# The last narrow block of gate and up, computed as one full mixed block and a half block multiplied directly

## The chip, the cores and the metric

The kernel runs on one core of a Trainium2 chip. The time is device microseconds (us) of one launch, the median of three runs. A profiled execution is a run of its own, with its own time. Engines are named as in the profile: PE (TensorE, matrix products; PEld is its weight load), DVE (VectorE), ACT (ScalarE), POOL (GpSimd) and SP (SyncE, which mostly issues DMAs).

## The reference

One decoder layer on x of 16 batches × 128 tokens × 1024 features, all in f32. Each of three parts normalises x, computes, and adds to x: a self-attention of width 256, a cross-attention with a softmaxed context, and a gated feed-forward with weights stored as 4-bit codes. The change is in the last:

```python
Wg = dequantize(gate_Wq, gate_scale, gate_zero)   # [2752, 1024], (code - zero) * scale
Wu = dequantize(up_Wq, up_scale, up_zero)         # [2752, 1024]
Wd = dequantize(down_Wq, down_scale, down_zero)   # [1024, 2752]
g = jnp.einsum('bsh,ih->bsi', x, Wg)
u = jnp.einsum('bsh,ih->bsi', x, Wu)
h = jax.nn.silu(g) * u
return jnp.einsum('bsi,hi->bsh', h, Wd)
```

So there are 2048 tokens, 1024 inputs, 2752 intermediate columns in each of gate and up, and 1024 outputs.

## The kernel before

The attention parts come first. Beside them DVE begins to dequantize weights and to store them, with the sums that are needed of them, in DRAM (`prepare`). The normalised rows are turned and stored in two halves of 1024 tokens, called passes here.

**Products with seven multiplications.** Where a product of 2 × 2 blocks would take eight block products, the kernel takes seven (Winograd's form of Strassen's scheme), at the price of sums of the operands and of the results. `GATE` (line 39) is the order of the seven for gate and up, `DOWN` (line 40) that for down. For gate and up the 2 × 2 blocks are two halves of the tokens (512 each), two halves of the inputs (512 each, four chunks of 128) and two halves of a block of columns. `BLOCKS` (line 41) cuts the 2752 columns into ten blocks of 2 × 128 and an eleventh of 2 × 96; the eleventh is `RB = 10` with half width `RW = 96`.

**First pass.** `one_block` (line 1084) computes each of the eleven blocks: 14 products, seven for gate and seven for up (`SEQUENCE`), each of four matmuls of 512 tokens into a PSUM bank (`products`, line 1044; the matmul is line 1063). A matmul call is two PE instructions in the profile. ACT copies partial results (`keep`), DVE adds, ACT applies Silu, DVE multiplies. The results h go to DRAM as `h_all[block, 1 or 2, token half]`. PE runs in an order written out by hand, and so does DVE here (`tensor` and `vector` are wrapped in `InOrder`). After each product `beside` (line 1383) does a step of other work: at first what is left of the attention (`tick`), then a step of `prepare`, and in the last block the operands of the second pass (`outer_operand`, `inner_right`).

**Weights.** `load_weights` (line 976) loads a tile of two products' weights, and runs `AHEAD = 4` tiles ahead of `next_tile`. Four tiles are loaded before the first block (line 1377), on SP's queue like nearly every load and store.

**Second pass.** For the ten full blocks the scheme is applied twice (`two_levels`, line 1190): blocks in pairs, 35 outer products (`OUTERS`), each with seven inner products of 256 tokens (their instructions stand under line 52, in the wrapper). POOL makes the weights' sums (`inner_left`, tiles li), DVE those of the tokens (`inner_right`, tiles ti), and `got` and `finish` put the results together on DVE and ACT. Those that serve several pairs (`KEPT`, line 1134) are made once, at the pair's first use: while outer product n runs, the sums for n + 1 go to the list `soon_due`, which is worked off between the inner products (`do_extra`), as is a second list, `extra`. After the outer products, `one_block` runs once more for the eleventh block, and at its end makes the four sums of h that down wants (`combine_h`, line 1013) from the first pass's h, reloaded into tiles hl, and its own. Sums of the last pair of full blocks that are left over are worked off by the second `beside` (line 1413), one after each product; at its third call that function also issues the first 25 loads of down (`operands`, line 902).

**Down.** Seven outer products (`DOWN`), each with seven inner products (`INNER`) of five pairs of full blocks, for which DVE makes the operands' sums (`combine`, line 1452). The eleventh block enters once per outer product with the tiles of `remainder` (line 1442), one more matmul pair in four of the inner products, which needs `h_all[10, q]` for that outer product's q.

**What sets the order.** Within an engine's stream, instructions that are not pinned in program order are placed by a planner that works with its own estimates; its costs are not shown. Its decisions can be read only from the order in the trace. SP's queue and POOL's are such streams. PE in down is one too.

Of the kernel before, what the change touches and what calls it, by code (L numbers as in the profile page):

```python
# [11 lines left out]
F32 = mybir.dt.float32  # L12
# [28 lines left out]
BLOCKS = [(b * 2 * P, min(P, (INTER - b * 2 * P) // 2)) for b in range(-(-INTER // (2 * P)))]  # L41

# [13 lines left out]
def decoder_layer(  # L56
# [100 lines left out]
    def load_raw(blk, mat, s):  # L157
# [10 lines left out]
        q, szs = (gq, gsz) if mat == "g" else (uq, usz)  # L168
        off = start + s * w
        raw = raw[:, : JC * w].rearrange("p (j f) -> p j f", j=JC)  # L170
        nc.sync.dma_start(raw, q[:, :, ds(off, w)])

        sz = pools["sz"].tile([P, 2 * P], F32, name="sz")[:, : 2 * w]
        nc.sync.dma_start(sz, szs[:, ds(2 * off, 2 * w)])
        scale, zero = (m.unsqueeze(1).to_broadcast([P, JC, w]) for m in (sz[:, :w], sz[:, w:]))
        return raw, scale, zero

    def prepare(jobs, ahead, queue, vector=nc.vector):


        units = [(blk, mat, s) for blk, mat in jobs for s in range(2)]
# [7 lines left out]
        for k, (blk, mat, s) in enumerate(units):  # L189
            w = BLOCKS[blk][1]  # L190
            size = [w, 512] if mat == "d" else [P, JC * w]
# [25 lines left out]
            yield  # L217
            if s == 0:
                continue
# [667 lines left out]

    RB = len(BLOCKS) - 1
    RW = BLOCKS[RB][1]
# [4 lines left out]
    h_all = {}  # L894

# [36 lines left out]
    with ExitStack() as gs:  # L932
# [9 lines left out]
        def attention_done():  # L942
# [5 lines left out]
            for blk in range(EARLY, len(BLOCKS)):  # L948
                jobs += [(blk, "g"), (blk, "u")]
                if blk >= EARLY + 2:  # L950
                    jobs.append((blk - EARLY - 2, "d"))
# [10 lines left out]
        SEQUENCE = [(mat, q) for mat in "gu" for q in GATE]  # L962

        def tiles_of(blk):
            todo = [(blk, *k) for k in SEQUENCE]
            return [todo[n : n + 2] for n in range(0, len(todo), 2)]
# [9 lines left out]
        def load_weights():  # L976
            if to_load:
                wt = cw.tile([P, 2, 512], F32, name="w")
                for n, (blk, mat, q) in enumerate(to_load.popleft()):
                    cols = slice(0, JC * BLOCKS[blk][1])  # L980
                    nc.sync.dma_start(wt[:, n, cols], wprep[blk, mat][GATE.index(q)])
                loaded.append(wt)
# [5 lines left out]
        def next_weights(w):  # L988
            if not waiting:
                wt = next_tile()  # L990
                waiting.extend(
                    wt[:, n, : JC * w].rearrange("p (j f) -> p j f", j=JC) for n in range(2)
                )
# [5 lines left out]
        def store(blk, q, half, t, delay=2):  # L999
            if (blk, q, half) not in h_all:  # L1000
                w = BLOCKS[blk][1]
                h_all[blk, q, half] = dram.tile(
                    [w, TB], F32, name=f"h{blk}_{q}{half}", tag=f"h{blk}_{q}{half}"
                )
            stores.append([delay, h_all[blk, q, half], t])
# [38 lines left out]
        def products(blk, mat, T, got):  # L1044

            w = BLOCKS[blk][1]
            bank, kept = {}, {}

            def keep(q, ps):
                t = kept[q] = ct.tile([P, TB], F32, name="k", tag=f"k{q}", bufs=2 if q == 1 else 1)  # L1050
                t = kept[q] = t[:w]
                nc.scalar.copy(t, ps)  # L1052

            def product(q):
                wt = next_weights(w)
                put_stores()
                first = {6: 1, 5: 1, 3: 1, 4: 7}.get(q, q)
                if first == q:
                    banks.rotate(1)
                    bank[q] = banks[0].tile([P, TB], F32, name=f"p{q}", tag="gu")[:w]  # L1060
# [23 lines left out]
        def one_block(ps, blk, T, between):  # L1084

            w = BLOCKS[blk][1]
            sg, hs, first_h = {}, {}, {}

            def gate(k, bank, add):
                t = sg[k] = ct.tile([P, TB], F32, name="sg", tag="sg")[:w]  # L1090
# [6 lines left out]
            def up(k, bank, add):  # L1097
                t = hs[k] = ch.tile([P, TB], F32, name="h", tag="h")[:w]
# [6 lines left out]
                if ps == 0:  # L1105
                    store(blk, 1 + n, half, t)
                    return
                if n == 1:
                    store(blk, 4, half, t)
                if (1 - n, half) in hs:  # L1110
                    for step in combine_h(
# [553 lines left out]
```

## Time and profile before

| | |
|---|---|
| time, median of 3 runs (lowest to highest) | 2329.98 us (2327.83 to 2329.99) |
| the profiled execution's own time | 2327.36 us |
| its span | 2325.4 us |
| PE busy | 2291.2 us, 99% |
| DVE, ACT, POOL busy | 1559.1, 557.3, 388.3 us |
| DMA | 424.69 MB, mean 183 GB/s |
| first pass, gate and up (from the wait for the first weights to the last block's end) | about 806 to 1370.8 us |
| of it the eleventh block | 1322.7 to 1370.8 us |
| second pass, outer products | 1370.8 to 1800.5 us |
| second pass, eleventh block | 1800.5 to 1848.6 us |
| down | 1848.6 to 2325.4 us |

Times in the trace count from the start of the span. A row of the timeline gives start, duration, engine, line, operation, tiles written and read, the count of instructions merged, and in brackets the engine's idle time before it with what ended it. PE's durations overlap, since matmuls are pipelined: what one costs is the step from one start to the next. A row of a table of waits gives who waited for whom, the total, how often, and the longest.

### The profile page before, as it was taken

What the parts mean: (1) busy time and instruction counts of PE and PEld (TensorE: products, weight loads), DVE (VectorE), ACT (ScalarE), POOL (GpSimd) and SP (SyncE); (2) the same over time, 40 slices, a digit from 0 to 9 for tenths busy, and PEclk for the clock granted to TensorE, in tenths of its full rate; (3) what the DMA queues carried; (4) which work ended last, traced back from release to release, by engine and by line L of the source; (5) the groups of instructions that cost most, each with busy time, mean ns of one, the idle gap of its engine ahead of it and who ended that gap; (6) DMA issues with size and microseconds to landing.
All of it is one profiled execution on the core that took longest, in us unless ns stands there. A gap on an engine that the chain in (4) does not pass through costs nothing.

```text
span 2325.4 us, 25297 instructions
## 1 busy us (share of the span) xinstructions
PE 2291.2 (99%) x8976; PEld 1585.3 (68%) x8976; DVE 1559.1 (67%) x2224; ACT 557.3 (24%) x891; POOL 388.3 (17%) x281
## 2 busy tenths in 40 slices
PE   8999999999999899999999999999999999999999
PEld 7556557667666564444444457888888488888888
DVE  6694788888888816776767547777777455443462
ACT  2111255565565551111111111222111100000000
POOL 5120122222222200000000023444443000000000
PEclk9999999999999999999999999999999999999999
DMA  6242365666676558787889733554554965434631
GB/s 242 66 132 89 109 172 172 179 183 181 180 220 207 166 147 260 253 286 258 276 265 317 249 95 98 198 173 140 196 195 131 322 193 160 158 124 146 218 113 37
DMA packets 275774, 424.69 MB, mean 183 GB/s; under 512 B 26752, under 2 KB 124928, under 8 KB 275520
## 3 DMA queue, kind: packets, MB, share of 16 engines
q1 hardware_dynamic: 256544, 398.16, 54.2%
q10 hardware_dynamic: 16800, 16.52, 2.3%
q0 software_dynamic: 2304, 8.39, 0.9%
q8 instruction: 72, 1.18, 0.2%
q14 instruction: 54, 0.44, 0.1%
HBM read 265.62 MB, written 157.35 MB: 182 GB/s over the span
## 4 chain that ended last, share of the span: by engine, by line
PE 93%; DVE 3%; DMA 1%; issue 1%; ACT 0%; SPq 0%; POOL 0%; DVEq 0%; ACTq 0%; POOLq 0%
PE p L1063 24%; PE po L1552 20%; PE q L52 17%; PE mm L52 11%; PE kq L52 8%; PE mm L367 5%; PE tr L52 3%; PE mm L382 2%; PE mm L263 2%; PE tr L314 1%; DMA kh<-kd 1%; DVE bnst L52 0%; DMA wo_again<-in_wo 0%; DVE kt L52 0%; DVE qmx L52 0%
## 5 line engine op out<-in xcount | busy, mean ns | idle before, releaser
L1063 PE MATMUL p<-b,w 128*128 128x512 f32 (+1 forms) x768 | 340.0, 595 | 6.0 <-DMA w<-wg 6.0
L1063 PEld LDWEIGHTS p<-b,w 128*128 128x128 f32 (+1 forms) x768 | 142.8, 186 | 191.7 <-issue 187.8
L1063 PE MATMUL p<-T,w 128*128 128x512 f32 (+1 forms) x576 | 255.5, 592 | 0.0
L1063 PEld LDWEIGHTS p<-T,w 128*128 128x128 f32 (+1 forms) x576 | 106.6, 186 | 138.7 <-issue 136.6
L52 PE MATMUL q<-ti,li 128*128 128x256 f32 x840 | 194.6, 382 | 4.2 <-DVE ti L52 4.2
L1552 PE MATMUL po<-wc,lc 128*128 128x256 f32 x840 | 183.4, 379 | 0.0
L52 POOL TENSOR_TENSOR li<-w 128x512 f32<-128x512 f32 x70 | 94.4, 1350 | 531.1 <-PE p L1063 476.5
L52 PEld LDWEIGHTS q<-ti,li 128*128 128x128 f32 x840 | 160.4, 191 | 27.4 <-issue 5.3
L1552 PEld LDWEIGHTS po<-wc,lc 128*128 128x128 f32 x840 | 159.6, 190 | 21.8
L683 POOL TENSOR_TENSOR qe<-qe,qden 128x1024 f32<-128x1024 f32 x64 | 121.6, 1899 | 266.8 <-DVE qden L52 231.8
L52 ACT COPY k<-q 128x512 f32<-128x512 f32 x105 | 61.4, 585 | 345.4 <-PE q L52 345.4
L52 DVE TENSOR_TENSOR pa<-pa,sz 128x512 f32<-128x512 int32 (+3 forms) x176 | 129.6, 737 | 5.5
L1552 PE MATMUL po<-wq,lq 128*128 128x256 f32 x560 | 126.7, 379 | 0.2 <-issue 0.2
L52 PE MATMUL mm<-kh,cxt 128*128 128x256 f32 x512 | 122.6, 382 | 3.6 <-DMA kh<-kd 3.3
L52 PE MATMUL kq<-cx,wk_sb 128*128 128x512 f32 x256 | 120.7, 594 | 4.0 <-ACT ke L640 3.5
L1052 ACT COPY k<-p 128x512 f32<-128x512 f32 (+1 forms) x72 | 42.1, 584 | 342.8 <-PE p L1063 342.8
L52 PEld LDWEIGHTS mm<-qs,m_sb 128*128 128x128 f32 x512 | 97.2, 190 | 38.9 <-issue 28.0
L52 PE MATMUL kq<-wq_sb,xn 128*128 128x512 f32 x256 | 120.5, 593 | 0.0
L52 PE MATMUL mm<-qs,m_sb 128*128 128x256 f32 x512 | 120.3, 379 | 0.0
L52 PEld LDWEIGHTS mm<-kh,cxt 128*128 128x128 f32 x512 | 95.9, 190 | 33.6 <-issue 19.6
L52 DVE TENSOR_REDUCE qmx<-kq 128x16 f32<-128x1024 f32 x64 | 76.3, 1193 | 63.0 <-PE kq L52 62.9
L1552 PEld LDWEIGHTS po<-wq,lq 128*128 128x128 f32 x560 | 106.0, 190 | 15.9 <-issue 0.8
(176 smaller groups left out, 3687.6 us busy)
## 6 DMA issues: line engine op xcount, KB each, us to landing
w<-wg SPq DMA_DIRECT2D x140, 256.0 KB, 3.0
w<-wu SPq DMA_DIRECT2D x140, 256.0 KB, 3.5
lq<-h SPq DMA_DIRECT2D x140, 256.0 KB, 4.5
kd<-kt SPq DMA_DIRECT2D x64, 512.0 KB, 3.5
kh<-kd SPq DMA_DIRECT2D x128, 256.0 KB, 5.5
h<-hc SPq DMA_DIRECT2D x80, 256.0 KB, 2.9
wq<-wd SPq DMA_DIRECT2D x70, 256.0 KB, 5.3
h<-h SPq DMA_DIRECT2D x60, 256.0 KB, 3.0
```

The source lines that it names most:

```text
L52: return lambda *args, **kw: self._tc.keep_in_program_order(fn(*args, **kw))
L263: tensor.matmul(ps, oT[:, d, ts(b % BPT, S)], wo_d[d][:, ts(h, 512)], start=(d == 0), stop=(d == 1),)
L314: nc.tensor.transpose(tr[:, j, :], xn[:, ts(4 * h + j, P)], ident)
L367: nc.tensor.matmul(ps[:, tokens], wqkv_sb[:, f, c, :], xnT[:, c, tokens], start=(c == 0), stop=(c == CC - 1),)
L382: nc.tensor.matmul(ps, xnT[:, c, ts(i, S)], wqkv_sb[:, 4:6, c, :], start=(c == 0), stop=(c == CC - 1),)
L683: nc.gpsimd.tensor_tensor(qe, qe, den.unsqueeze(2).to_broadcast(wide), ALU.mult)
L1052: nc.scalar.copy(t, ps)
L1063: nc.tensor.matmul(ps, wt[:, j, :], T[q][:, j, :], start=(first == q and j == 0), stop=(q in (2, 3, 4) and j == JC - 1), skip_group_check= ...
L1552: nc.tensor.matmul(bank[:, i, :], l[:, ts(i, S)], w,  start=(start and c == 0 and i % 2 == 0), stop=(stop and c == len(pairs) - 1), skip_g ...
```

## The change

The eleventh block is split in another way. Of gate's 192 columns and of up's 192, the first 128 of each form one block of full width ("m"): gate's 128 are its first half, up's 128 its second. It takes seven products instead of fourteen. The 64 + 64 columns left (`REST`) form a single tile of 128 columns ("r"), which is multiplied directly: `half_product` runs four times, for two token halves and two halves of the inputs, using the token block T[5] = (block − T[1]) so that the second half of the tokens can be added to a copy of the first. In "r" the rows of gate and up lie in different partitions: gate's 64 rows go through Silu and are shifted by a DMA on ACT's queue from partitions 0 to 63 to partitions 64 to 127, and there multiplied with up's. Columns are ordered accordingly on the host, and `prepare` has one unit for "r" and two for "m" in place of four.

The sums of this block's h for down are no longer made at the end of the second pass. All its h go to DRAM (the second pass's under the keys "e" and 4), and `last_combinations` loads them in down's first outer product, once after its inner product 7 and once after 3, makes the sums on DVE and stores them from ACT's queue.

With the block shorter, the calls of `between` change: nine per block instead of fourteen, two after parts of "r" and one after each product of "m". `beside`'s work is keyed to those. Down's first loads still come at the third call.

Two more edits: the first tile of weights of the first pass is loaded from POOL's queue instead of SP's, and the sums `inner_right(T, 4)` are put on the list `extra` in outer product n = 4, where before they came with n = 5.

The diff, cut to its core:

```diff
+RB = len(BLOCKS) - 1
+RW = BLOCKS[RB][1]
+REST = 2 * RW - P
+SUBS = [(start + s * w, w) for start, w in BLOCKS[:RB] for s in range(2)]
+SUBS += [(BLOCKS[RB][0], P), (BLOCKS[RB][0] + P, REST)]
...
+        if mat == "r":
+            parts = [(m, *SUBS[-1]) for m in "gu"]
+        elif mat == "m":
+            parts = [("gu"[s], *SUBS[-2])]
+        else:
+            parts = [(mat, start + s * w, w)]
+        at = 0
+        for m, off, w in parts:
+            q, szs = matrices[m]
+            nc.sync.dma_start(raw[:, :, ds(at, w)], q[:, :, ds(off, w)])
...
-        units = [(blk, mat, s) for blk, mat in jobs for s in range(2)]
+        units = [(blk, mat, s) for blk, mat in jobs for s in range(1 if mat == "r" else 2)]
...
+            if mat == "r":
+                out = wprep[blk, mat] = dram.tile([2, *size], F32, name="wr0", tag="wr0")
+                for n in range(2):
+                    stores.append((out[n], A[0, n]))
...
-                jobs += [(blk, "g"), (blk, "u")]
+                jobs += [(blk, mat) for mat in ("gu" if blk < RB else "rm")]
...
+        LAST = [("r", n) for n in range(2)] + [("m", q) for q in GATE]
         def tiles_of(blk):
-            todo = [(blk, *k) for k in SEQUENCE]
+            todo = [(blk, *k) for k in (SEQUENCE if blk < RB else LAST)]
...
-        def load_weights():
+        def load_weights(queue=nc.sync):
             if to_load:
                 wt = cw.tile([P, 2, 512], F32, name="w")
-                for n, (blk, mat, q) in enumerate(to_load.popleft()):
-                    cols = slice(0, JC * BLOCKS[blk][1])
-                    nc.sync.dma_start(wt[:, n, cols], wprep[blk, mat][GATE.index(q)])
-                loaded.append(wt)
+                todo = to_load.popleft()
+                for n, (blk, mat, q) in enumerate(todo):
+                    queue.dma_start(wt[:, n], wprep[blk, mat][q if mat == "r" else GATE.index(q)])
+                loaded.append((wt, len(todo)))
...
-                if ps == 0:
-                    store(blk, 1 + n, half, t)
-                    return
-                if n == 1:
-                    store(blk, 4, half, t)
-                if (1 - n, half) in hs:
-                    for step in combine_h(
-                        blk,
-                        half,
-                        first_h[1, half],
-                        first_h[2, half],
-                        hs[0, half],
-                        hs[1, half],
-                        vector,
-                    ):
-                        step()
...
+            make = {"g": products(T, gate), "u": products(T, up)}
             for n, (mat, q) in enumerate(SEQUENCE):
                 make[mat](q)
-                if ps == 1 and n == 5:
-                    hl = xres.tile([P, 2, 2, TB], F32, name="hl", tag="X6")
-                    for half in range(2):
-                        for k in (1, 2):
-                            t = first_h[k, half] = hl[:w, k - 1, half]
...
                 between(n, mat, q)
+        def last_block(ps, T, between):
+            keys = {0: (1, 2), 1: ("e", 4)}[ps]
+            bank, up, done = {}, {}, {}
+            todo = deque()
+            def put(half, t, first, row, n):
+                parity = keys[n]
+                store(RB, parity, half, t[first], row=row)
+            def small(half, x, u):
+                g = ct.tile([P, TB], F32, name="sg", tag="sg")
+                nc.scalar.activation(g[:REST], x[:REST], AF.Silu)
+                nc.scalar.dma_start(g[ds(REST, REST)], g[:REST])
+                def mult():
+                    rows = ds(REST, REST)
+                    t = ch.tile([P, TB], F32, name="h", tag="h")
+                    vector.tensor_tensor(t[rows], u[rows], g[rows], ALU.mult)
+                    put(half, t, rows, 0, 1)
+                todo.append(mult)
+            def half_product(p, w, q, start, stop):
+                for j in range(JC):
+                    nc.tensor.matmul(
+                        bank[p],
+                        w[:, j, :],
+                        T[q][:, j, :],
+                        start=(start and j == 0),
+                        stop=(stop and j == JC - 1),
+                        skip_group_check=True,
+                    )
+            put_stores()
+            ws = [next_weights() for _ in range(2)]
+            for p in range(2):
+                banks.rotate(1)
+                bank[p] = banks[0].tile([P, TB], F32, name=f"p{p}", tag="gu")
+            half_product(0, ws[0], 1, True, False)
+            k = ct.tile([P, TB], F32, name="k", tag="k1", bufs=2)
+            nc.scalar.copy(k, bank[0])
+            between(0, "r", 0)
+            half_product(1, ws[1], 2, True, True)
+            c0 = ct.tile([P, TB], F32, name="sg", tag="sg")
+            vector.tensor_tensor(c0, bank[1], k, ALU.add)
+            small(0, c0, c0)
+            put_stores()
+            half_product(0, ws[0], 5, False, False)
+            between(1, "r", 1)
+            half_product(0, ws[1], 3, False, True)
+            small(1, bank[0], bank[0])
+            def finish(half, t):
+                put(half, t, slice(0, RW), 0, 0)
+                put(half, t, slice(RW, P), REST, 1)
+            def got(k, ps, add):
+                n, half = k
+                if k == (1, 1):
+                    t = up[half] = ch.tile([P, TB], F32, name="h", tag="h")
+                    vector.tensor_tensor(t, ps, add, ALU.add)
+                elif k == (1, 0):
+                    t = ch.tile([P, TB], F32, name="h", tag="h")
+                    vector.tensor_tensor(t, ps, add, ALU.add)
+                    vector.tensor_tensor(t, t, done[half], ALU.mult)
+                    finish(half, t)
+                else:
+                    t = done[half] = ct.tile([P, TB], F32, name="sg", tag="sg")
+                    if add is None:
+                        nc.scalar.activation(t, ps, AF.Silu)
+                        vector.tensor_tensor(t, up[half], t, ALU.mult)
+                        finish(half, t)
+                    else:
+                        vector.tensor_tensor(t, ps, add, ALU.add)
+                        nc.scalar.activation(t, t, AF.Silu)
+            make = products(T, got)
+            for n, q in enumerate(GATE):
+                make(q)
+                between(2 + n, "m", q)
+                if todo:
+                    todo.popleft()()
...
                     soon_due.extend(inner_right(T, OUTERS[n + 1][1]))
                 if n == 0:
                     extra.append(lambda: outer_operand(T, 4))
+                elif n == 4:
+                    extra.extend(inner_right(T, 4))
...
-        for _ in range(AHEAD):
-            load_weights()
+        for n in range(AHEAD):
+            load_weights(nc.gpsimd if n == 0 else nc.sync)
...
             if blk == RB:
-                for k in {("g", 1): (5,), ("g", 2): (7,), ("u", 6): (6,)}.get((mat, q), ()):
+                for k in {("r", 0): (5,), ("r", 1): (7,), ("m", 6): (6,)}.get((mat, q), ()):
                     outer_operand(T1, k)
-                if (mat, q) == ("u", 1):
+                if (mat, q) == ("m", 1):
                     for step in inner_right(T1, 1):
                         step()
...
             if blk == RB:
                 blocks.update(pass1)
-            one_block(0, blk, T, beside)
+                last_block(0, T, beside)
+            else:
+                one_block(blk, T, beside)
...
-        one_block(1, RB, T1, beside)
+        last_block(1, T1, beside)
...
+        def last_combinations(half):
+            h = {}
+            for q in (4, "e", 1, 2):
+                h[q] = dh.tile([P, TB], F32, name="dh")[:RW]
+                nc.sync.dma_start(h[q], h_all[RB, q, half])
+            for q, dst, a, b, op in (
+                (5, 4, "e", 4, ALU.add),
+                (7, "e", 1, "e", ALU.subtract),
+                (6, 1, 4, 1, ALU.subtract),
+                (3, 2, 2, 1, ALU.subtract),
+            ):
+                nc.vector.tensor_tensor(h[dst], h[a], h[b], op)
+                new_h(RB, q, half)
+                nc.scalar.dma_start(h_all[RB, q, half], h[dst])
...
                 ps = bank[set_]
                 multiply(ps, pairs, set_ == iq, iq == 6 or more is not None)
                 put_outs()
+                if n == 0 and iq in (7, 3):
+                    last_combinations(0 if iq == 7 else 1)
...
     order = np.concatenate(
-        [start + s + 2 * np.arange(w) for start, w in BLOCKS for s in range(2)]
+        [start + s + 2 * np.arange(w) for start, w in BLOCKS[:RB] for s in range(2)]
+        + [BLOCKS[RB][0] + np.r_[0 : 2 * RW : 2, 2 * REST + 1 : 2 * RW : 2, 1 : 2 * REST : 2]]
     )
-    subs = [(start + s * w, w) for start, w in BLOCKS for s in range(2)]
```

## The prediction

> **What bounds the kernel now.** I read the page first: its busy line, then the chain that ended last.
>
> ```profile
> span 2325.4 us, 25297 instructions
> ...
> PE 2291.2 (99%) x8976; PEld 1585.3 (68%) x8976; DVE 1559.1 (67%) x2224; ACT 557.3 (24%) x891; POOL 388.3 (17%) x281
> ...
> PE 93%; DVE 3%; DMA 1%; issue 1%; ACT 0%; SPq 0%; POOL 0%; DVEq 0%; ACTq 0%; POOLq 0%
> ```
>
> TensorE is the bound nearly everywhere: 34 us of idle in the span, 93% of the chain. So a matmul removed is time removed, unless its stage then starves. Busy time alone does not say so for one stage; the table by stretch does. Its columns are the stretch, its length, then PE, PEld, DVE, ACT, POOL busy (instructions), granted clock, DMA share and GB/s. These are the last block of gate and up in the first pass, the outer products, that block in the second pass, and down:
>
> ```profile
> 1322.70:1370.80 48.10, 48.10 (x114) 18.50 (x113) 16.95 (x17) 5.97 (x10) 10.03 (x7) 1.00 0.30 96
> 1370.80:1800.50 429.70, 425.45 (x1961) 373.12 (x1960) 312.32 (x405) 82.52 (x129) 178.50 (x134) 1.00 0.48 158
> 1800.50:1848.60 48.10, 48.10 (x114) 18.28 (x113) 19.52 (x31) 7.03 (x11) 0.00 (x0) 1.00 0.92 325
> 1848.60:2325.40 476.80, 472.15 (x2185) 414.11 (x2183) 241.23 (x376) 8.10 (x8) 0.00 (x0) 1.00 0.46 148
> ```
>
> In both last blocks PE is busy without a gap. DVE has 30 us to spare in each; DMA is at 0.30 in the first and at 0.92 in the second, where down's first operands arrive. Next, PE's own waits and the timeline at the two largest that the diff touches:
>
> ```profile
> PE p L1063 <- DMA w<-wg: 6.0, 1, 6.0
> PE q L52 <- DVE ti L52: 4.2, 2, 3.4
> ```
> ```profile
> 811.99 5.36 PE L1063 MATMUL p<-b,w 128*128 128x512 f32 x8 [6.01 <-DMA w<-wg]
> 823.24 3.60 PE L1063 MATMUL p<-b,w 128*128 128x512 f32 x8
> ...
> 1434.01 3.62 PE L52 MATMUL q<-ti,li 128*128 128x256 f32 x16
> 1449.82 5.38 PE L52 MATMUL q<-ti,li 128*128 128x256 f32 x16 [3.44 <-DVE ti L52]
> ```
>
> Each stall costs more than its gap: eight 512-column matmuls take 5.36 us after it and 3.60 us otherwise, sixteen of 256 columns 5.38 against 3.62, so 1.76 us more each time. Who holds the first load back is on the SP and POOL queues:
>
> ```profile
> 799.21 8.98 SPq L654 DMA_DIRECT2D kd<-kt  x2
> 808.23 2.09 SPq L981 DMA_DIRECT2D w<-wg  x3
> ```
> ```profile
> 801.56 1.90 POOL L683 TENSOR_TENSOR qe<-qe,qden 128x1024 f32<-128x1024 f32 x1 [7.67 <-DVE qden L52]
> 810.37 0.62 POOL L755 DMA_DIRECT2D x_all<-X  x1 [6.91 <-DVE X L52]
> ```
>
> SP stands at its second kd store, issued at 807.67, until DVE has made kt; the first weights go out only after it. POOL is idle from 803.46 to 810.37.
>
> **What the Trainium skill says.** "TensorE: Matmul & The Clock Gate", section "Back-to-back issue gap": a warm matmul takes about N/2.4 + 2.5 ns, N being the columns that stream through, so 216 ns for 512; the width of the stationary tile is not in it. The trace agrees: 112 instructions in 48.07 us (1800.53 to 1848.60) are 429 ns each, twice that for these f32 operands, and the 96-wide block costs what a 128-wide one does. Section "What's actually happening" of the same page: after about 3.4 us of idleness the array runs at half clock for about as long; the 1.76 us are that, and the gap of 0.81 us at 1409.76 cost 0.07 (3.69 against 3.62). "DMA: Bandwidth & Descriptors", section "Anatomy of one DMA — SWDGE (gpsimd) path": a DMA's wait is served on the issuing sequencer before dispatch, which is what SP shows, and a DMA from POOL takes about 2.0 us + bytes/436 GB/s, an estimate of 2.6 us for 256 KB; the trace's own POOL stores of 512 KB took 5.0 and 6.0 us to land, so I take 3.5 us.
>
> **The change, part by part.**
>
> *Products.* Before, a last block is 14 products of 4 matmul calls, each call two instructions: 112. After, 7 products of the mixed block (gate's 128 columns as one half, up's as the other) and 4 half products for the 64 + 64 left over: 11 × 8 = 88. Saved: 24 instructions × 0.429 us = 10.3 us per pass, 20.6 us in both.
>
> *Work beside them.* Per pass the half block adds one PSUM copy, one add, two Silu on 64 rows, two multiplies and two 128 KB shifts across partitions on ACT's queue, some 0.6 us an operation. They lie beside 37.8 us of matmuls, and ACT (6 of 48 us) and DVE (17 to 20) have room. Each multiply is traced at least 3.4 us of products behind its shift; the stores I see landing take 2.4 to 3.5 us, so DVE should not stand there. If it did, the mixed block's evictions queue behind it, with banks to spare. The copy of the first half product must end before its bank is added to; a half product of 3.43 us lies between. Price 0; uncovered, the worst is one shift and Silu, 4 us a pass.
>
> *Preparation.* 24 dequantizing operations and 8 combinations on 384 columns become 18 and 4 on 512, and 14 stores become 9; the last preparation on DVE is at 1312, before the last block begins at 1322.7, and one step less is wanted. The last block also calls it 6 times, not 9, with nothing left to call. Price 0; if it were late, each remaining unit (six operations of 0.4 to 0.7 us, about 4 us) would stand before the outer products.
>
> *Combinations for down.* Eight 0.68 us DVE operations and eight 192 KB stores leave the end of the second pass, with its four 192 KB loads; eight loads, eight operations and eight stores (ACT's queue) come into down's first product, 68.7 us long with DVE busy 44.4. The first user is the remainder of down's third product, loaded from 68.7 us on. At the end of the block this helps: before, those operations delayed the operands of down's second inner product to 1857.3, just as PE reached it (1857.23), and SP's next five weights to 1853.79. PE did not wait, so I credit nothing.
>
> *Prefetch.* Down's 25 first loads are placed after the third `beside` call: before, 12 calls into the block (10.3 us), now 20 (17.2 us). They went out from 1811.90 to 1828.87, 17.0 us. At worst, issue ends at 17.2 + 17.0 = 34.2 us and lands 5.4 us later at 39.6, with the block ending at 37.8. But the first inner product (8.6 us) takes only the first 15 tiles, landed by 33; the next needs tiles up to 20 (36.4) and 5.2 us of DVE, 41.6 against 46.4. Price 0.5 us for a slip here, between 0 and 6.8 (5 us of wait and the half clock).
>
> *`inner_right(T, 4)` moved* from the sixth outer product to the fifth (n = 4): four DVE operations at a pitch of 0.60. In the sixth DVE runs without a break from 1437.51, and the third `ti` (1448.99) is what PE waits for at 1446.38. Gone: 3.44 + 1.76 = 5.2 us. In the fifth one moved operation comes before the `ti` needed at 1434.01: its start moves from 1432.92 to 1433.52, its end to 1434.2, a slip of 0.2 to 0.3. Net 4.9. The Silu that follows moves later too, but DVE's h multiplies start 0.3 us later at most, and 2.4 us are gone behind them.
>
> *First weights from POOL's queue.* Two 256 KB loads leave SP, where they stood behind kd. POOL's order is the planner's, which is not shown. If it puts them after the multiply of 801.56, they issue at about 803.5 and land at 807.0: wait 1.0 instead of 6.01, half clock spared, 6.7 us gained. From the other side: landed before 805.97 would give 7.8; placed behind x_all (810.37) they issue at 811.0, land at 814.5, and cost 2.5. I take 6.7, since on SP these loads stood before the kh loads that wait for kd's landing, so they were counted ready no later than X is. What comes next on PE holds: the pieces 8 to 15 us on read kh landed before 800, and the second kh (821.03) is used at 834.43, or 827 then. x_all goes out after the load and `T<-b,T` waits for it, but is not needed until the sixth product.
>
> *Sum.* 20.6 + 4.9 + 6.7 − 0.5 = 31.7 us. Of the profiled span 2325.4 that leaves 2293.7; 2.0 us lie around it (2327.36), so 2295.7. The median of the runs is 2.6 above that execution: **2298.3 us**.
>
> **Rivals.**
> 1. *The load is placed behind x_all on POOL.* For it: x_all stands earlier in the program. Against: it waits for X at 808.8 to 810.1. Loses 6.7 + 2.5: 2307.5.
> 2. *The DVE wait only moves*, to the fifth outer product or the evictions of the sixth, since DVE is at 312 of 430 us there and runs there without a break twice. No 4.9: 2303.2.
> 3. *Down starves at its start*: DMA ran at 0.99 from 1800 to 1838, and now has 10 us less. 6.8 instead of 0.5: 2304.6.
> 4. *Slower.* The new loads of the last rows stand on SP behind a load whose buffer is not yet free, and DVE has the combinations at its head, so the evictions of down's inner products wait. In that stretch SP's longest wait on DVE's lc was 14.4 us, in the whole trace 31.5. PE gives 10.3 us of slack (one inner product). Two halves at the longest: 2 × (31.5 − 10.3 + 1.8) = 46 us: 2344. It decides from about 27 us per half; the planner saw these waits, which speaks against it.
>
> **How the numbers follow.** Measurements of this kernel tell 0.2% (4.7 us) from no change. Likeliest 0.58 (2298.3, itself 2294.5 to 2302); rival 1 0.18, rival 2 0.08, rival 3 0.09: all faster. Rival 4 with smaller mishaps: 0.04 slower, 0.03 within. Range 2294.5 (every stall gone) to 2309.5 (rivals 1 and a small slip): it leaves out rival 4 and pairs of rivals. Faster 0.93, same 0.03, slower 0.04.
>
> **What would show it.** PE 8928 matmuls; last blocks of 37.8 us with no gap; the first weights on POOL before x_all, and the first product near 807 with 3.6 us for eight; no gap at the sixth outer product; down's first inner product following the block at once, with no PE gap in its first outer product. I am wrong if the gaps return elsewhere, above all at down's start.

## The result, and the profile after

The changed kernel takes **2296.7 us** (median of four, 2295.1 to 2297.1) against 2328.9 us of the kernel before on the same chip: ratio 0.986, 95% interval 0.984 to 0.988. The profiled execution is 2296.27 us with a span of 2294.5. The forecast was 2298.3 us, and 2295.7 for the profiled execution.

The busy line from the page of the changed kernel:

```profile
span 2294.5 us, 25166 instructions
...
PE 2269.7 (99%) x8928; PEld 1581.6 (69%) x8928; DVE 1554.0 (68%) x2210; ACT 555.4 (24%) x887; POOL 389.2 (17%) x283
```

48 matmul instructions are gone, two times 24, and PE has 25 us of idle left in place of 34. The table by stretch of the changed kernel, with the same columns and for the same four stages as in the prediction:

```profile
1317.05:1354.82 37.77, 37.77 (x90) 16.72 (x89) 14.81 (x15) 4.20 (x7) 6.22 (x4) 1.00 0.31 93
1354.82:1779.85 425.03, 424.00 (x1962) 371.96 (x1961) 314.29 (x405) 83.20 (x130) 182.06 (x136) 1.00 0.49 161
1779.85:1817.61 37.76, 37.76 (x89) 16.72 (x88) 16.93 (x27) 5.25 (x8) 0.00 (x0) 1.00 0.97 340
1817.61:2294.50 476.89, 472.16 (x2185) 414.10 (x2183) 242.63 (x377) 8.70 (x9) 0.00 (x0) 1.00 0.48 155
```

Each last block went from 48.1 to 37.8 us with PE busy throughout. The outer products went from 429.7 to 425.0. Down is as long as it was (476.9 and 476.8), though it now makes the sums of the last rows as well and DMA in the block ahead of it rose to 0.97. PE's waits, and PE's timeline where the two stalls were:

```profile
PE q L62 <- DVE ti L62: 1.0, 2, 0.8
PE p L1087 <- DMA w<-wg: 0.7, 1, 0.7
```
```profile
807.99 3.67 PE L1087 MATMUL p<-b,w 128*128 128x512 f32 x8 [0.73 <-DMA w<-wg]
...
1418.37 3.69 PE L62 MATMUL q<-ti,li 128*128 128x256 f32 x16 [0.18 <-DVE ti L62]
...
1430.76 3.62 PE L62 MATMUL q<-ti,li 128*128 128x256 f32 x16
```

The wait for the first weights is 0.73 us instead of 6.01, and the eight matmuls behind it run at full speed. The third `ti` of the sixth outer product is there in time (1430.76, no wait); what is left there is 0.18 us in the fifth. The other 0.8 us in that row of waits stands at an earlier outer product and was there before the change (0.81). POOL's queue shows why the weights are early:

```profile
804.69 1.18 POOL L1012 DMA_DIRECT2D w<-wg  x2
811.65 0.54 POOL L780 DMA_DIRECT2D x_all<-X  x1 [5.79 <-DVE X L62]
```

The two loads of the first tile go out behind the multiply (802.85) and ahead of x_all, as the prediction took it; they land at 807.86 and 808.49. Last, PE where down begins:

```profile
1814.18 3.60 PE L1087 MATMUL p<-b,w 128*128 128x512 f32 x8
1817.61 8.80 PE L1663 MATMUL po<-wq,lq 128*128 128x256 f32 x40
1826.25 4.05 PE L1663 MATMUL po<-wc,lc 128*128 128x256 f32 x18
```

Down follows the block at once, and its second inner product follows the first.

### The profile page after: what moved, and what is told of

Its sections match the earlier page's. It is cut to its first block, busy times and chain, and to the rows that moved or that the text cites. A ratio compares the mean times of both kernels' runs of the same rounds, so it can differ in the third digit from the quotient of the medians.

```text
span 2294.5 us, 25166 instructions
## 1 busy us (share of the span) xinstructions
PE 2269.7 (99%) x8928; PEld 1581.6 (69%) x8928; DVE 1554.0 (68%) x2210; ACT 555.4 (24%) x887; POOL 389.2 (17%) x283
## 4 chain that ended last, share of the span: by engine, by line
PE 94%; DVE 3%; DMA 1%; issue 1%; ACT 0%; SPq 0%; POOL 0%; DVEq 0%; POOLq 0%; ACTq 0%
PE p L1087 23%; PE po L1663 21%; PE q L62 18%; PE mm L62 11%; PE kq L62 8%; PE mm L392 5%; PE tr L62 3%; PE mm L407 2%; PE mm L288 2%; PE p L1162 1%; PE tr L339 1%; DMA kh<-kd 1%; DVE bnst L62 0%; DVE qden L62 0%; DMA wo_again<-in_wo 0%
## 5 line engine op out<-in xcount | busy, mean ns | idle before, releaser
L1087 PE MATMUL p<-b,w 128*128 128x512 f32 x704 | 310.4, 592 | 0.7 <-DMA w<-wg 0.7
L1087 PEld LDWEIGHTS p<-b,w 128*128 128x128 f32 x704 | 133.4, 190 | 167.1 <-issue 162.8
L1087 PE MATMUL p<-T,w 128*128 128x512 f32 x528 | 234.2, 592 | 0.0
L1087 PEld LDWEIGHTS p<-T,w 128*128 128x128 f32 x528 | 100.1, 190 | 124.6 <-issue 123.1
L62 POOL TENSOR_TENSOR li<-w 128x512 f32<-128x512 f32 x70 | 96.1, 1374 | 514.6 <-DMA w<-wu 476.8
L62 DVE TENSOR_TENSOR pa<-pa,sz 128x512 f32<-128x512 int32 (+1 forms) x172 | 129.0, 750 | 5.4
L392 PE MATMUL mm<-xnT,wqkv_sb 128*128 128x512 f32 (+1 forms) x320 | 113.2, 510 | 0.0
```

Source lines behind the costliest of these rows:

```text
L62: return lambda *args, **kw: self._tc.keep_in_program_order(fn(*args, **kw))
L392: nc.tensor.matmul(ps[:, tokens], wqkv_sb[:, f, c, :], xnT[:, c, tokens], start=(c == 0), stop=(c == CC - 1),)
L1087: nc.tensor.matmul(ps, wt[:, j, :], T[q][:, j, :], start=(first == q and j == 0), stop=(q in (2, 3, 4) and j == JC - 1), skip_group_check= ...
```

## The experiments

Times are medians of four runs where nothing else is said; the kernel before took 2328.4 us beside the first four kernels and 2329.2 beside the next four. "First product" is the first of gate and up.

### The parts one by one

**e1: the first weights on SP again.**

```diff
-            load_weights(nc.gpsimd if n == 0 else nc.sync)
+            load_weights(nc.sync)
```

> The changed kernel with the first tile of weights on SP's queue again; everything else stays. Theory: this edit alone was worth the wait of 6.01 us less the 0.73 us that is left, and the half clock of 1.7 us behind it: 7.0 us. The wait of about 6 us at the first product comes back with eight matmuls in 5.2 to 5.4 us, and the time is 2296.7 + 7.0 = 2303.7 us (2302 to 2305). Rival 1: the load is not what bounds the first product, and the attention stage before it takes back what the load gives (PE came to the first product 1.3 us later after the change); then 2296.7 + 4 or less, 2300 or below. Rival 2: the later loads, which move up on SP's queue without this tile, matter too; then other waits change as well, and it costs more than 8 us.

Measured: 2302.2 us (2301.0 to 2302.8), ratio 0.989 (0.987 to 0.990). PE's timeline of e1:

```profile
811.54 6.12 PE L1087 MATMUL p<-b,w 128*128 128x512 f32 x8 [6.02 <-DMA w<-wg]
817.50 3.62 PE L62 MATMUL mm<-qs,m_sb 128*128 128x256 f32 x16
```

The wait is back at 6.02 us, and eight matmuls take 5.96 us (817.50 − 811.54) against 3.51. The outer products (425.0 us) and the later stages are untouched. So neither rival holds: the load is what bounds that product, and no other wait of that size appeared. By the trace the edit is worth 5.3 + 2.4 = 7.7 us from the start of that wait on. The two profiled executions differ by 6.0 us of span, because the changed kernel lost 1.7 us in the stage before that e1 did not lose (below); the medians show 5.5.

**e2: `inner_right(T, 4)` made with n = 5 again.**

```diff
-                elif n == 4:
-                    extra.extend(inner_right(T, 4))
```

> The changed kernel with inner_right(T, 4) taken from outer product n = 4, so that it is made with n = 5 as before; everything else stays. Theory: the gap of 3.44 us before the third ti of the sixth outer product is back, with 5.38 us for sixteen matmuls behind it, and the 0.25 us of slip in the fifth is gone: 4.95 us, 2296.7 + 4.95 = 2301.6 us (2300.5 to 2303). Rival (the DVE wait only moves): another wait ends the stage, and the outer products take as long as in the changed kernel, 425.0 us: 2296.7 us.

Measured: 2299.9 us (2297.3 to 2301.5), ratio 0.988 (0.986 to 0.989). PE's timeline of e2:

```profile
1427.75 1.97 PE L62 MATMUL q<-b,li 128*128 128x256 f32 x8
1433.15 5.31 PE L62 MATMUL q<-ti,li 128*128 128x256 f32 x16 [3.43 <-DVE ti L62]
```

The gap is back, the sixteen matmuls behind it take 5.31 us (5.38 before the change), and the outer products take 429.52 us instead of 425.03: 4.5 us. DVE's wait did not move somewhere else in the changed kernel; it is gone. The median lies 0.6 us below the expected range: 3.2 us over the changed kernel, where the profiled executions show 3.8. Of the 4.5 us, 0.7 went the other way ahead of the first product, which starts at 807.27 here and at 807.99 there.

**e3: the eleventh block alone**, with both edits above undone.

> The changed kernel with both side edits undone: first tile of weights on SP, inner_right(T, 4) with n = 5. What is left is the eleventh block itself, with its combinations for down. Theory: 24 instructions of 0.429 us less in each of two passes, nothing else: 20.6 us under the kernel before, 2328.9 - 20.6 = 2308.3 us (2307 to 2310), both stalls as in the kernel before, down following the block at once. Rival (the parts help each other: the block's gain reaches the end only with the stalls gone): more than 2312 us. Rival (the side work of the half block, or down's loads, cost something that the side edits hide): a gap in one of the two last blocks or in down's first outer product.

Measured: 2306.4 us (2304.9 to 2307.7), ratio 0.991 (0.989 to 0.992), 22 us under the kernel before, where 20.6 were expected; the runs' spread of 3 us is larger than that difference. The table by stretch of e3, for the outer products and the block of the second pass:

```profile
1361.36:1790.95 429.59, 425.33 (x1962) 373.19 (x1960) 313.09 (x405) 83.22 (x130) 180.51 (x136) 1.00 0.48 160
1790.95:1828.71 37.76, 37.76 (x89) 16.72 (x88) 17.02 (x27) 5.25 (x8) 0.00 (x0) 1.00 0.95 333
```

Both stalls are there (the outer products are as long as in the kernel before, and the first product waits 5.99 us), and each block takes 37.77 us without a gap. The traces of the kernel before and of e3 differ by 20.0 us of span: 20.6 from the blocks, less 0.85 since more of the half clock after the first wait fell on matmuls here (eight in 6.05 us against 5.20), and 0.25 spread over the rest. The parts add up, 22.0 + 6.5 (from e3 to e2) + 4.2 (from e3 to e1) = 32.7 against 32.2 and 33.2 measured for all three in two sets of runs; so within the runs' spread none helps or hides another.

**e4: the load of the first weights pinned behind x_all on POOL's queue**, the first rival made on purpose.

```diff
-            nc.gpsimd.dma_start(x_all[b], X[b])
+            xa = nc.gpsimd.dma_start(x_all[b], X[b])
+            if b == B - 1:
+                tc.keep_in_program_order(xa)
...
-                    queue.dma_start(wt[:, n], ...)
+                    d = queue.dma_start(wt[:, n], ...)
+                    if queue is nc.gpsimd:
+                        tc.keep_in_program_order(d)
```

> The changed kernel with the load of the first tile pinned on POOL's queue behind the x_all store that it passes in the changed kernel; this is the first rival of the prediction, made on purpose. Theory: the load is issued after x_all at about 812.2 us and lands 3.2 us later (804.69 to 807.86 in the changed kernel): the first product starts at 815.5, 7.5 us later than at 807.99, and runs at half clock for 1.7 us: 9.2 us more than the changed kernel, 2305.9 us (2304 to 2308). The queue's place decides the sign of this edit: slower than leaving the load on SP (2303.7). Rival (the landing is set by something else than the place in the queue, for instance by the traffic that other loads make): less than 4 us more, 2300.7 or below.

Measured: 2310.8 us (2307.7 to 2311.8), ratio 0.992 (0.990 to 0.994): slower than with the load on SP, as expected, but by 8.6 us in the medians instead of 2, and above the expected range. POOL's timeline of e4:

```profile
814.49 0.62 POOL L780 DMA_DIRECT2D x_all<-X  x1 [6.91 <-DVE X L62]
815.10 0.56 POOL L1014 DMA_DIRECT2D w<-wg  x1
```

The load landed at 820.60, 5.5 us after its issue; in the changed kernel it took 3.2 (804.69 to 807.86). Beside it in e4 are x_all's store and the kh loads that SP issues from 815.02 on; that they are what slowed it was not tested. PE waited 10.64 us, then took 6.06 us for eight matmuls. Against the changed kernel that is 9.9 + 2.55 = 12.5 us from the edit. Of the other 3.0 us of the 15.5 between the two profiled executions, 2.8 arose before 707.1 us, where e4 had longer waits for a cx load and for kh; whether the pins have a part in those isn't known. Against e1 the edit itself is 4.7 us.

### Prices that the sum put at nothing

**e5: down's first loads 20 us later in the program.**

```diff
-            if n == 2:
+            if n == 8:
                 prefetched.append(operands(DOWN[0]))
```

> The changed kernel with the 25 first loads of down placed at the ninth call in the eleventh block of the second pass instead of the third, some 20 us later in the program; it is for the third rival, down starving at its start. The planner puts five stores of h among the loads that stood behind them. Theory: the loads run from about 1802 to 1819 us instead of 1791.6 to 1809.1, the first fifteen tiles land by 1816 and the rest by 1824, and the sums for down's second inner product end near 1827, where PE wants them at 1826.25: 0 to 1.5 us more, 2296.7 to 2298.2 us. So the start of down has some 10 us to spare. Rival (down's start is on the edge already): a gap of 5 us or more in down's first two inner products and the half clock after it, 2303.5 us or more.

Measured: 2295.6 us (2295.1 to 2296.8), against 2296.0 for the changed kernel run beside it. PE's timeline of e5 where down begins:

```profile
1816.87 8.80 PE L1663 MATMUL po<-wq,lq 128*128 128x256 f32 x40
1825.51 4.70 PE L1663 MATMUL po<-wc,lc 128*128 128x256 f32 x21
```

No gap. The planner did not move the loads by 20 us: counted from the start of the block, the first was issued 1.6 us later than in the changed kernel, and the last 7.4 us later (at 1815.35, 36.2 us into the block, instead of 28.9). The first fifteen had landed at 1812.71 and the last at 1820.76, after the start of down at 1816.87. So down's start bears loads that come some 6 to 7 us later, and the third rival had no room.

**e9: more work on DVE in down's first outer product.** Behind each of the eight sums two (and in the second kernel five) operations that leave the tile as it is:

```diff
                 nc.vector.tensor_tensor(h[dst], h[a], h[b], op)
+                for _ in range(2):
+                    nc.vector.tensor_tensor(h[dst], h[dst], h[dst], ALU.max)
```

> The changed kernel with each of the eight sums for down followed by two more DVE operations of the same size that change nothing (the maximum of a tile with itself): 16 x 0.6 = 9.6 us more on DVE in down's first outer product, where it is busy 45.75 of 68.69 us in the changed kernel. It is for the price of nothing that the prediction put on these sums. Theory: they are covered by 23 us of spare time; no gap of PE in down's first two outer products (68.69 us each), 2296 us (2293.5 to 2298). Rival (they stand at DVE's head, and the evictions behind them are what PE waits for): a gap of 2 us or more in one of the two.

> The same with five more operations behind each sum: 40 x 0.6 = 24 us more, so that DVE would be busy 69.8 us of the 68.69. Theory: this is about where the cover ends: the evictions in the second half of the first outer product come up to 12 us late, one inner product of PE is 8.6 us, so a gap of 1 to 6 us at the next use of an eviction's bank, 2297 to 2303 us. If there is no gap even here, the next product's spare time (35.8 busy of 68.7 us) takes what is left over, and the price of nothing is safe; if the gap is 10 us or more, the sums are nearer to the edge than the busy time says.

Measured, one execution each: 2294.9 us and 2294.5 us; down took 476.8 and 477.4 us (476.9 in the changed kernel). The table by stretch of the second, for about down's first and second outer product:

```profile
1816.00:1885.00 69.00, 68.96 (x320) 60.30 (x319) 61.76 (x110) 2.16 (x3) 0.00 (x0) 1.00 0.71 224
1885.00:1953.00 68.00, 68.00 (x317) 59.77 (x316) 43.41 (x69) 1.01 (x1) 0.00 (x0) 1.00 0.63 203
```

DVE has 16 us more in the first and 7.6 more in the second stretch, and PE waited for no operand. The expected edge isn't there: what did not fit ran over into the second product. The price of nothing holds with five more operations behind each sum. That is for the place that the planner gave the sums (1853.6 to 1866.3 us in the changed kernel), behind the operands of the first inner products; the fourth rival's condition, sums ahead of those operands on DVE, was not tried.

### What a stall costs beside its gap

**e7: work in the wait.** The kernel of e1 (weights on SP), with six matmuls on operands that are there already, ahead of the first product and into the bank that it then starts anew:

```diff
+                if not warmed:
+                    warmed.append(1)
+                    for _ in range(6):
+                        nc.tensor.matmul(
+                            ps, T[q][:, 0, :P], T[q][:, 0, :], start=True, stop=True,
+                            skip_group_check=True,
+                        )
                 for j in range(JC):
                     nc.tensor.matmul(
```

> The changed kernel with the first weights on SP (as e1) and, ahead of the first product, six matmuls of 512 columns on operands that are there already, into the bank that the first product then starts anew: 6 x 0.857 = 5.1 us of work in the wait of 6.0. Theory (part of what a stall costs is the half clock after idleness, not the wait): the weights still land at the same time, so the first product starts where it did in e1 (811.5 us, give or take the length of the attention stage), but its eight matmuls take 3.5 us in place of 5.96: 2302.2 - 2.4 = 2299.8 us (2298.5 to 2301.5). Rival (the slow matmuls come from something else, the weights' arrival one by one or the first use of the bank): eight matmuls take 5 us or more, and the time is that of e1, 2302 us, or up to 5 us more where the added work delays the first product.

Measured: 2301.6 us (2298.7 to 2303.7); the runs spread over 5 us, so their median doesn't decide it. The trace does. PE's timeline of e7:

```profile
805.25 4.46 PE L1091 MATMUL p<-b 128*128 128x512 f32 x10
810.48 3.70 PE L1096 MATMUL p<-b,w 128*128 128x512 f32 x8 [0.77 <-DMA w<-wg]
814.01 3.62 PE L62 MATMUL mm<-qs,m_sb 128*128 128x256 f32 x16
```

Five of the six fill the wait (ten instructions; the sixth ran before the kh matmuls), the weights come as late as in e1 (the first product starts 109.0 and 109.1 us after the same matmul near 702 us), and the eight matmuls take 3.53 us (814.01 − 810.48) where e1 took 5.96. The bank's first use is now by the added matmuls, and they show no slowness either (ten in 4.46 us, the last one's tail included). The granted clock was 1.00 over the eight matmuls here and 0.59 in e1. So the slow matmuls after a wait come from PE's idleness and from nothing in the weights or the bank.

### The part that was not in the sum

**The changed kernel again**, since PE came to the first product 1.3 us later than before the change.

> The changed kernel once more, beside the next three, as what they are compared with. It also tells which part of the attention stage's length is chance: in the first profile the eight matmuls after the wait for kh at 699 us ran at half clock for 1.3 us (a step of 3.02 us between two groups that take 1.72 otherwise) after a gap of 2.16 us, while two other runs with gaps of 2.44 and 1.92 us show none of it. If it is chance, the stage up to the first product takes 805.5 to 807.5 us here and the time stays within 2295 to 2299 us; if the change makes it, the first product starts at 807.9 to 808.1 us again.

Measured: 2296.0 us (2293.5 to 2296.5), ratio 0.986 (0.984 to 0.987). In its profiled execution the first product starts at 808.04, so by what was written this speaks for the change as the cause. The other traces speak against: PE's work up to there is the same in all of these kernels and in the same order (e7's added matmuls aside), and the first product's distance from the end of the second group below, near 704 us, is the same 103.4 to 103.8 us in all that have the load ahead of x_all. The difference is made at one place, shown here in PE's timeline of the changed kernel (first profile):

```profile
699.00 2.40 PE L62 MATMUL mm<-kh,cxt 128*128 128x256 f32 x8 [2.16 <-DMA kh<-kd]
701.20 3.18 PE L62 MATMUL kq<-cx,wk_sb 128*128 128x512 f32 x4
```

Four matmuls of 512 columns take 3.02 us there (701.20 to the next start at 704.22) where 1.72 is usual. From the start of the first group to the end of the second it is 3.5 us in the kernel before, e1, e3, e7 and the second e9 (gaps of 1.92, 2.44, 1.74, 1.74 and 1.79 us), and 5.1 to 5.2 in both profiles of the changed kernel, e2, e5 and the first e9 (gaps of 2.16, 2.38, 2.41, 2.44 and 2.31); in e4 it is 6.3, after a gap of 3.24. A gap of 2.44 us is in both lists, so the gap's length alone does not decide. What decides is shown in the last section: how much of the gap falls into one of the windows by which the clock is set, and these windows lie differently in every execution. Kernels that do the same up to 800 us fall on both sides, so the change alone does not make it.

**e8: that gap has the cause of the first one.** SP's timeline of the changed kernel, then that of e8:

```profile
681.74 0.52 SPq L679 DMA_DIRECT2D kd<-kt  x1
688.95 0.33 SPq L653 DMA_DIRECT2D cxt<-in_cxt  x1
689.38 1.80 SPq L683 DMA_DIRECT2D kh<-kd  x4
```
```diff
-            nc.sync.dma_start(ct, cxt[b])
+            (nc.gpsimd if b == batches[B - 2] else nc.sync).dma_start(ct, cxt[b])
```

> The changed kernel with one more load taken from SP's queue: the fifteenth cxt, at which SP stands from 682.3 to 688.95 us while kd for the kh loads behind it has landed at 684.92; it goes to POOL's queue. It is the same cause as the first product's wait in the kernel before: a load whose operands are there stands behind one that waits. Theory: the kh loads are issued at 685.0 instead of 689.38 and land by 694.5, the gap of 2.16 us at 699 us goes, and with it the half clock that sometimes follows: 2.2 to 3.9 us less than the changed kernel, about 2294 us (2292.5 to 2295.5). Rival (the DMAs are the limit there, not the queue's order): kh lands no more than 1 us earlier, 2296 us. Rival (POOL stands at the load in SP's place and its multiply comes late): a new wait at the transposes of qe, 2297 us or more.

```profile
681.27 0.53 SPq L681 DMA_DIRECT2D kd<-kt  x1
684.54 1.75 SPq L685 DMA_DIRECT2D kh<-kd  x4
```

Measured: **2291.9 us** (2291.8 to 2292.6), ratio 0.984 (0.983 to 0.986), 4.1 us under the changed kernel run beside it. The kh loads go out at 684.54 instead of 689.38, as soon as kd has landed (684.46), all four have landed by 691.75 instead of 698.87, the wait at 699 us is gone, no new wait stands at the transposes of qe, and the first product starts at 803.48. So neither rival holds; the gain is slightly more than the 2.2 to 3.9 us expected. It beats both kernels, and its runs lie closer together (0.8 us) than those of the changed kernel (3.1), which fits a half clock that comes only in some runs.

## Why the prediction was right, step by step

The landmarks of the two first profiles, in us; a minus is time saved.

| step | predicted | measured | how |
|---|---|---|---|
| products, two passes | −20.6 | −20.6 | 48.07 to 37.77, twice |
| `inner_right` moved | −4.9 | −4.7 | outer products 429.73 to 425.03 |
| first weights from POOL | −6.7 | −7.0 | wait 6.01 to 0.73, eight matmuls 5.20 to 3.51 |
| slip at down's start | +0.5 | 0 | no gap |
| arrival at the first product | not in it | +1.3 | 1.7 of half clock after kh, 0.4 earlier until there |
| sum | −31.7 | −31.0 | spans: −30.9 |

**Products.** Right to the hundredth: 88 instructions at 0.429 us are 37.8 us. e3 shows this part alone, without help from the others.

**Work beside them.** Price nothing was right, one step in it was wrong: "DVE should not stand there". In the second pass the shifts took 4.6 and 6.4 us from issue to landing (1792.58 to 1797.20, 1794.40 to 1800.84), not the 2.4 to 3.5 that I took from stores elsewhere, and DVE stood 4.29 and 2.20 us for them. DMA was at 0.97 there; in the first pass, with DMA at 0.31, they took 2.2 and 3.9 us and DVE did not wait for them. PE never waited for what queued up behind.

**Prefetch.** I placed the loads where the program has them, 17.2 us into the block. The planner issued the first at 1791.62, 11.8 us in, and the last at 1808.70, 28.9 us in, so the worst case of 34.2 us did not come. The slip of 0.5 was a hedge and should have been 0; e5 shows that loads 6 to 7 us later are still covered.

**`inner_right`.** The stall of 3.44 us went with its half clock and came back in e2. The slip that I set at 0.2 to 0.3 is seen as 0.18 and a few tenths more in the inner products behind it.

**First weights.** Order on POOL and size as said; the size holds for the half clock of the kernel before, and against e1, where more of it fell on matmuls, the same edit is worth 7.7 us. The landing took 3.2 us for an estimated 3.5; "DMA: Bandwidth & Descriptors" of the Trainium skill, section "Anatomy of one DMA — SWDGE (gpsimd) path", gives an estimate of 2.6 by its formula for this size, and the measured 3.2 here and 5.5 in e4 decide: both lie above the formula, the second with other transfers beside it. The first rival (2307.5) was priced with a landing of 3.5 us; made in e4, where it took 5.5, it came to 2310.8, of which some 3 us arose earlier.

**What was missing** is that a stage left alone may vary. The 1.3 us of later arrival turned 0.6 us more gain than forecast into 0.7 less in the profiled execution; in the medians the gain is 32.2 against 31.7 forecast. So the parts are right each by itself, but that the profiled execution came within 0.6 us of its forecast is in part luck: two misses of opposite sign. Of the 1.6 us by which the median lies under 2298.3, 1.1 is the kernel before, which took 2328.9 us beside it and not 2329.98.

## What to carry to other kernels

On SP's queue one blocked transfer held back loads whose sources were ready: PE waited 6 us for that at the first product, and the kh loads of e8's place went out 4.5 us late. Look, at each large wait for a DMA, for when its source was ready and what stood ahead of it on the issuing queue. Moving one load to a queue that is idle at that moment paid 7 us here and 4 us more at a second place (e8), and placing the same load behind the wrong neighbour cost 4.7 us of the trace against not moving it (e4). And price a stall of TensorE with the slow matmuls after it, 1.7 to 2.55 us here: removing the gap pays for both.

## What the runs showed of the hardware that was not expected

**Half clock after short gaps.** "TensorE: Matmul & The Clock Gate" of the Trainium skill, section "What's actually happening", speaks of an idle window of about 3.4 us that runs freely, so that the phase matters. The traces hold the moments at which the granted clock changed, and agree on the window: the stretches at half clock last 3.41, 6.82 or 13.65 us (one, two and four windows), and within each trace the changes lie whole windows apart. But a whole window need not be idle. Two neighbouring windows of the changed kernel (first profile), then two of e1, at the wait for kh; after the length stands PE's busy time, and the granted clock is the third number from the end:

```profile
696.98:700.39 3.41, 1.39 (x7) 1.26 (x8) 3.20 (x6) 1.06 (x1) 0.00 (x0) 1.00 1.06 335
700.39:703.80 3.41, 3.41 (x7) 1.69 (x6) 1.16 (x2) 0.00 (x0) 0.00 (x0) 0.50 1.07 396
```
```profile
693.60:697.01 3.41, 2.93 (x22) 1.45 (x20) 1.61 (x3) 2.64 (x6) 1.90 (x1) 1.00 1.08 226
697.01:700.42 3.41, 1.45 (x7) 1.33 (x8) 3.31 (x5) 1.06 (x1) 0.00 (x0) 1.00 1.04 312
```

In the changed kernel 2.02 us of a gap of 2.16 fall into one window, and the next window runs at half clock. In e1 the edge of a window cuts a longer gap, of 2.44 us, into 0.48 and 1.96, and the clock stays. All twelve traces are sorted by this: at the wait for kh the idlest window had 2.02 to 2.41 us without a matmul in the six that lost clock (the changed kernel twice, e2, e4, e5, the first e9), and 1.32 to 1.96 in the five that had a gap there and did not (the kernel before, e1, e3, e7, the second e9). The rest of these traces agrees: once the clock is full, no window with less than 2.02 us of idleness is followed by half clock, and every one with more is. So for this mix of work the edge lies near 2.0 us of a window of 3.41.

Where the windows lie against the program differs from execution to execution (the first stretch at full clock begins 12.0 to 15.0 us after the span's start), and that alone can move a time by 1.7 us. Both profiles of the changed kernel fell on the slow side, so no two profiles of one kernel show both.

**The loss after a long wait depends on the windows too.** After waits of 6.0 us, eight matmuls took 5.20, 5.96 and 6.05 us in three kernels, and 6.06 after one of 10.6: 1.7 to 2.55 us above 3.51. The half clock itself lasted the same 6.82 us in those three (13.65 in e4), but began at different moments of the wait. Of the time after the wait, 3.40 us in the kernel before, 4.94 in e1, 5.11 in e3 and 5.15 in e4 lay in it, and half of that is the loss. A window at half clock in which PE still idled for 1.13 us or more did not end it (e1's had 1.89 us, e3's 1.71, e4's 1.13 and 1.68); one with at most 0.15 us did. The 1.76 of the prediction was the low end.
